# Six batches of an attention result turned by VectorE and DMA instead of TensorE, a fixed order in layer 2, and the last two groups of seven products interleaved

## The chip, the cores and the metric

The kernel runs on one core of a Trainium2 chip. The metric is device time in microseconds (us) of one execution; lower is better. The core has five engines that run side by side and wait for each other by semaphores: TensorE (PE in the profile: matrix products and transposes into PSUM), VectorE (DVE), ScalarE (ACT), GpSimd (POOL) and SyncE (SP), which here only issues transfers. Transfers that SP issues stand in one queue, in order; ScalarE can issue transfers on a queue of its own.

## The reference, cut to what matters

Four layers act on x, 8 batches of 128 tokens with 512 features, all in 32-bit floats:

```
x = x + L0_ffn(L0_cond(x))      # gated MLP with low-rank adapters, then a routed adapter layer
x = x + L1_ffn(L1_cond(x))      # adapters
x = x + L2_ffn(L2_cond(x))      # attention over a paged cache, then a mixture with 8 experts
x = x + L3_ffn(L3_cond(x))      # routed adapters, then 64 experts of rank 8, the best 16 gated
```

The change touches what follows the attention of layer 2. Attention gives y2 with tokens on the partitions; the rest of layer 2 needs it with features on the partitions:

```
H       = y2 @ W.T + b                       # 512 x 512
z       = y2 @ A                             # rank 32
weights = routing(H[anchors, :8], z[anchors] @ LiMEs.T)   # anchors: every second token
x       = x + H + (z * (weights @ LiMEs)) @ Bmat * 0.5
```

and the end of layer 3, where the gated ranks z (512 by 1024 tokens, called zgT) are multiplied by a 512 x 512 matrix and added to x, which is then the output.

## The kernel before, in words

Attention (`attention`, called through `att.run`) takes 32 steps: eight quarters of the heads (`qd`, 0 to 7), and within each four pairs of batches (`p`, 0 to 3), so step n = 4 qd + p. A step projects the next step's queries, keys and values, weighs (scores `st`, L1249, and the exponentials on ScalarE), sums and mixes (`av`, L1301). The sums of the exponentials are inverted on VectorE (`inverted`), written to memory and read back as R, spread over all partitions (L1293 and L1294 on SP); R scales `av` into oT (`divided`, L1311). One step later `leave(n - 1)` multiplies oT with the output weights (L1055, tiles wo_one, wo_two, wo_six) and adds into y2; the last sums of it are added on GpSimd (L1336, L1341), in the last step on VectorE. After the last quarter (`qd` = 7) a pair's y2 is complete when its `leave` is done: the pair p - 1 in the step of pair p.

Products of size 2 x 2 blocks are made with seven block products and sums of blocks instead of eight products (`seven`, and in the last layer the class `Seven`).

At the end of steps 29, 30 and 31 (qd = 7, p = 1, 2, 3) `end.turn` turns the two batches of the pair before: four transposes on TensorE for each batch into one PSUM bank (L1884), copied by VectorE or ScalarE to Y2T (L1885). The last two batches are turned in `layer2`. After step 31 `run` scales the last pair (`divided`), makes the sums of blocks of it (`outputs`, four VectorE sums), starts the first quarter of H on TensorE (`end.product(0, ...)`: two PSUM banks, 16 products), and then does the last `leave`. `layer2` turns batches 6 and 7, makes the anchors' logits (`anchors`, tile hdT) and z (`low`), the products for the quarters 0 to 3 of the tokens (`product`), with `routing` on VectorE beside them, and the addition to x (`added`).

An fp32 product of TensorE stands in the trace as two instructions ("passes").

A planner orders the instructions of each engine ahead of time; it may put an instruction that is ready ahead of an earlier one that is not. `kept(...)` (`tc.keep_in_program_order`) exempts an instruction from that: the kept ones of an engine stay in the order in which the program gives them. In attention nearly everything is kept; in `ending` before the change the transposes of `turn`, the products of `low`, `anchors` and `product`, and all of layer 3 are not. SP's queue within a step is, in order: the turned new keys and queries (`written`, L1204, four transfers), their loading (L1237, L1239), the sums and R (L1293, L1294), the turned cached keys (L1204) and their loading (kT, L1200). In step 30 the loads of W2 and Aw follow (L1873, L1877); after step 31 come the weights of the last two layers (`open3`, L2024 to L2041) and the sums read back for a check (L833). The tiles called kn hold gathered keys of the cache and belong to the pool `kvp`, two buffers; no keys are gathered from step 30 on.

PSUM has eight banks. In attention and layer 2 they are three with the tag st, two with av and three with mm; in layer 3 all eight have the tag mm.

At the end, `layer3` turns zgT for the second half of the tokens, begins the two last groups (`last_begun(1, k)`), makes the sums zs on VectorE and does `last(1, 0)` and `last(1, 1)`: the six remaining block products of a group (`go_on`, L2121, L2122, L2124 on VectorE between them), additions to x (L2252), and for each of the four results an addition from PSUM (L2258) and a store from SP's queue (L2259). The result blocks (0, 0) and (1, 0) of a group share one PSUM bank, (0, 1) and (1, 1) the other.

Of the kernel before, what the change touches and what calls it, by code (L numbers as in the profile page):

```python
# [47 lines left out]
def forward(ctx: ExitStack, tc: tile.TileContext, a: dict, out: bass.AP):  # L48
# [32 lines left out]
    late_turned = w3T, wB3T, A2T  # L81
# [795 lines left out]
def attention(tc, a, x, ident, lens, kvrow, part, ww, wop, ypool, sums, rot, eps, psa, c2, chunks, mm):  # L877
# [524 lines left out]
    def run(pool_, end_of, bank, keep):  # L1402
# [12 lines left out]

        def some(ops, k=1):
            return lambda: [next(ops, None) for _ in range(k)]

        for n, (qd, p) in enumerate(steps):
# [75 lines left out]
            if qd == NQ - 1 and p:  # L1495
                for j in range(2):
                    end.turn(y2, 2 * (p - 1) + j, bank)
        divided(n)
        every(outputs(n))
        end.product(0, ("st", "st"), bank)  # L1500
# [313 lines left out]
def ending(  # L1814
# [64 lines left out]
    def turn(y2, b, bank):  # L1879
        if not Y2T:  # L1880
            Y2T.append(early.tile([P, DC, NT], F32, tag="yT", name="y2T"))
        ps = bank("mm", [P, DC, P], f"y2T_{b}")
        for c in range(DC):
            pe.transpose(ps[:, c, :], y2[:, b, c * P : (c + 1) * P], ident)  # L1884
        (act.copy if b % 2 else dve.tensor_copy)(Y2T[0][:, :, b * P : (b + 1) * P], ps)  # L1885

# [3 lines left out]
    def low(bank):  # L1890

        ps = bank("mm", [P, NT // 4], "z2")
        for c in range(DC):
            for q in range(4):
                mmq(ps[slot(q), :], A2[:, c, :], Y2T[0][:, c, quarter(q)], c == 0, c == DC - 1)
        act.copy(zq, ps)

    def anchors(bank, meanwhile):

        ps = bank("mm", [P, P], "hdT")  # L1900
        for c in range(DC):
            for q in range(4):
                mmq(ps[slot(q), :], WH[:, c, :], Y2T[0][:, c, q * NT // 4 + 1 : (q + 1) * NT // 4 : 2], c == 0, c == DC - 1)
        hdT = L3.w3.tile([P, P], F32, tag="hdT", name="hdTs")
        dve.tensor_copy(hdT, ps)
        meanwhile()
        ps = bank("mm", [P, NA, 32], "hd")
        pe.transpose(ps.rearrange("p q e -> p (q e)"), hdT, ident)
        dve.tensor_tensor(hd, ps[:, :, 0:16], b16.unsqueeze(1).to_broadcast([P, NA, 16]), ALU.add)
# [8 lines left out]
    def product(q, tags, bank, at=range(2), begun=False):  # L1918

        for i, tag in zip(at, tags):  # L1920
            ps = H[q, i] if begun else bank(tag, [P, 2, NT // 4], f"h_{q}_{i}")
            for o in range(2):
                for c in range(DC):
                    mmq(
                        ps[:, o, :], W["2"][:, c, (2 * i + o) * P : (2 * i + o + 1) * P], Y2T[0][:, c, quarter(q)],
                        not begun and o == 0 and c == 0, begun and c == DC - 1,
                    )
            H[q, i] = ps
# [166 lines left out]
    class Seven:  # L2095


        def __init__(self, name, bank, A, B):
            self.A, self.B = A, B
            self.even, self.odd = (bank("mm", [P, 2, 256], f"{name}_{i}") for i in range(2))  # L2100
            self.p1, self.u = (
                L3.w3.tile([P, 256], F32, tag=f"seven_{n}", name=f"{n}_{name}", bufs=2) for n in ("p", "u")
            )
            self.c = {(0, 0): (self.even[:, 0], None), (0, 1): (self.odd[:, 1], self.u),
                      (1, 0): (self.even[:, 1], self.u), (1, 1): (self.odd[:, 0], self.p1)}
# [5 lines left out]
        def begin(self):  # L2111
            self.into(self.even[:, 0], self.A[0], self.B[0], True)
            act.copy(self.p1, self.even[:, 0])

        def go_on(self):
            a11, a12, a22, s1, s2, s3, s4 = self.A
            b11, b21, b22, t1, t2, t3, t4 = self.B
            u, p1, even, odd = self.u, self.p1, self.even, self.odd
            self.into(odd[:, 1], s1, t1, True)
            self.into(odd[:, 0], s2, t2)  # L2120
            dve.tensor_tensor(u, odd[:, 0], p1, ALU.add)  # L2121
            dve.tensor_tensor(p1, odd[:, 1], p1, ALU.add)  # L2122
            self.into(even[:, 1], s3, t3)
            dve.tensor_tensor(p1, even[:, 1], p1, ALU.add)  # L2124
            self.into(odd[:, 1], s4, b22)
            self.into(even[:, 0], a12, b21)
            self.into(even[:, 1], a22, t4)
# [111 lines left out]
    def last_begun(g, k, bank):  # L2239

        f = S["o", g, k] = Seven(f"o3_{g}_{k}", bank, S["b"][k], S["z", g])
        f.begin()

    def last(g, k):
        f = S["o", g, k]
        f.go_on()
        for (i, j), (ps, more) in reversed(f.c.items()):
# [3 lines left out]
            if more is not None:  # L2251
                dve.tensor_tensor(t, t, more, ALU.add)  # L2252
        for ij in ((1, 1), (0, 1), (0, 0), (1, 0)):
            ps = f.c[ij][0]
            o = 2 * k + ij[0]
            tok = slice(g * 512 + ij[1] * 256, g * 512 + (ij[1] + 1) * 256)
            t = x[:, o, tok]
            dve.tensor_tensor(t, ps, t, ALU.add)  # L2258
            sp.dma_start(out[o * P : (o + 1) * P, tok], t)  # L2259

    def layer2(y2, bank, do=range(NB)):

        for b in do:
            turn(y2, b, bank)
        anchors(bank, lambda: low(bank))
        where = ["mm"]
        folding = fold_scores(lambda tag, shape, name: bank(where[0], shape, name))
        if (0, 0) not in H:
# [18 lines left out]
    def layer3(bank, between=lambda behind: None):  # L2287
# [33 lines left out]
        last(1, 0)  # L2321
        last(1, 1)
# [3 lines left out]
        product=product, shifted=shifted, open3=open3, layer2=layer2, layer3=layer3,  # L2326
# [66 lines left out]
```

## Time and profile before

| what | value |
|---|---|
| median of 3 runs | 1475.64 us (1473.62 to 1477.49) |
| profiled execution | 1473.67 us |
| its span, first to last instruction | 1471.8 us |
| TensorE busy | 1459.9 us, 99% of the span |
| VectorE busy | 1066.8 us, 72% |
| GpSimd busy | 855.2 us, 58% |
| ScalarE busy | 559.0 us, 38% |
| granted clock of TensorE | 0.999 |

Busy times of engines overlap. Of the engine that is busy nearly all the time, every wait counts; idle time of the others costs nothing by itself. "L1884" is line 1884 of the kernel before the change. A number in the trace such as "[3.19 <-DMA R<-sums]" is the idle time of that engine ahead of the instruction, and what ended it.

### The profile page before, as it was taken

Reading aid. Unit: us, or ns where it says so; the run is one execution under the profiler, and the core shown is the slowest. Engines: PE = TensorE matmul, PEld = TensorE weight load, DVE = VectorE, ACT = ScalarE, POOL = GpSimd, SP = SyncE. Lnnn points to the kernel's source line nnn. Section 1 sums busy time; section 2 is a strip of 40 time slices with the busy share of each in tenths; the row PEclk is TensorE's granted clock in tenths of the full one; section 3 lists DMA queues with packets and bytes.
Section 4 is the critical chain, followed back from the end, with each engine's and each line's share of the span. In section 5 each row is a group of like instructions: output and inputs, shape, how many; then the busy total and the mean of one; then the engine's idle time right before and its main releaser. Section 6 shows DMA issues by size and latency. Waiting matters only on the chain.

```text
span 1471.8 us, 17654 instructions
## 1 busy us (share of the span) xinstructions
PE 1459.9 (99%) x5333; PEld 921.6 (63%) x5333; DVE 1066.8 (72%) x2128; ACT 559.0 (38%) x1416; POOL 855.2 (58%) x877
## 2 busy tenths in 40 slices
PE   9999999999999999999999999999999999999998
PEld 7888786455555555555565555556555555657886
DVE  4675535488878887877778787777878788875575
ACT  1111101044445544454554445455444444542110
POOL 2231104477767777777677777767777776731310
PEclk9999999999999999999999999999999999999999
DMA  7430312214655544464454456444445544343001
GB/s 244 131 76 26 73 35 70 90 39 123 178 157 165 156 121 129 150 184 129 136 151 120 126 157 184 129 137 150 117 129 155 173 137 134 115 122 99 1 9 52
DMA packets 178488, 177.02 MB, mean 120 GB/s; under 512 B 72336, under 2 KB 148208, under 8 KB 178256
## 3 DMA queue, kind: packets, MB, share of 16 engines
q1 hardware_dynamic: 160208, 138.79, 32.7%
q0 software_dynamic: 17056, 36.49, 8.0%
q8 instruction: 45, 0.74, 0.2%
q10 hardware_dynamic: 1120, 0.52, 0.1%
q14 instruction: 59, 0.48, 0.1%
HBM read 132.36 MB, written 43.11 MB: 119 GB/s over the span
## 4 chain that ended last, share of the span: by engine, by line
PE 91%; DMA 3%; DVE 3%; POOL 1%; issue 1%; ACT 0%; SPq 0%; ACTq 0%; DVEq 0%; POOLq 0%
PE st L1249 17%; PE av L1301 16%; PE g L414 9%; PE q_six L1055 8%; PE q_one L1055 5%; PE q_five L1055 5%; PE wo_two L1055 5%; PE dn L414 5%; PE wo_one L1055 4%; PE wo_six L1055 4%; PE eo_l L53 3%; PE h L1834 2%; PE z L1834 2%; PE o L1834 1%; PE midp_l L53 1%; DMA qT<-turned_new 1%
## 5 line engine op out<-in xcount | busy, mean ns | idle before, releaser
L998 POOL DMA_INDIRECT kn<-in_k_cache,kvrow_k x256 | 270.8, 1058 | 77.7 <-issue 67.1
L998 POOL DMA_INDIRECT vals<-in_v_cache,kvrow_v x256 | 273.1, 1067 | 73.6 <-issue 49.5
L1301 PE MATMUL av<-pT,vals 128*128 128x512 f32 x640 | 290.6, 593 | 0.2 <-DVE oT L1311 0.2
L1253 ACT ACTIVATE pT<-st,hide 128x512 f32<-128x512 f32 x256 | 175.9, 687 | 187.2 <-PE st L1249 187.1
L1249 PE MATMUL st<-qT,kT 128*128 128x512 f32 x512 | 236.2, 594 | 1.5 <-DMA qT<-turned_new 1.4
L1301 PEld LDWEIGHTS av<-pT,vals 128*128 128x128 f32 x640 | 121.6, 190 | 152.9 <-issue 146.9
L1154 POOL TENSOR_TENSOR vq<-q,txq 128x256 f32<-128x256 f32 x128 | 121.1, 977 | 131.5 <-ACT sqq L1128 89.9
L1249 PEld LDWEIGHTS st<-qT,kT 128*128 128x128 f32 x512 | 96.4, 190 | 111.2 <-issue 99.0
L1269 DVE TENSOR_TENSOR part<-pT 128x512 f32<-128x512 f32 x128 | 88.4, 691 | 77.6 <-ACT pT L1253 73.5
L1055 PE MATMUL q_one<-q,x 128*128 128x384 f32 x256 | 93.1, 486 | 0.0
L1128 ACT ACTIVATE sqq<-q 128x128 f32<-128x128 f32 x252 | 78.2, 310 | 11.8 <-DVE q L1104 5.1
L1055 PEld LDWEIGHTS q_one<-q,x 128*128 128x128 f32 x256 | 48.6, 190 | 39.7 <-issue 14.1
L1055 PE MATMUL q_six<-q_s,xs_all 128*128 128x384 f32 x192 | 69.8, 486 | 0.0
L1109 ACT COPY q<-q_one 128x256 f32<-128x256 f32 x32 | 11.9, 372 | 148.8 <-PE q_one L1055 142.7
L1055 PE MATMUL wo_one<-o,oT 128*128 128x256 f32 x256 | 65.7, 379 | 0.0
L1249 PE MATMUL st<-qT,kTn 128*128 128x512 f32 x128 | 65.4, 593 | 0.0
L1055 PE MATMUL wo_two<-o_s,os 128*128 128x256 f32 x256 | 60.6, 380 | 0.0
L1253 ACT ACTIVATE pT<-st,rs 128x512 f32<-128x512 f32 x64 | 44.0, 687 | 38.6 <-PE st L1249 38.6
L483 POOL TENSOR_TENSOR ws<-wu 128x256 f32<-128x256 f32 (+1 forms) x9 | 6.4, 711 | 87.7 <-DMA wu<-in_WuT 87.7
L1055 PEld LDWEIGHTS wo_one<-o,oT 128*128 128x128 f32 x256 | 48.7, 190 | 13.3 <-issue 0.5
L1285 ACT COPY rows<-rows 32x32 f32<-32x32 f32 x96 | 20.7, 216 | 93.1 <-DVE rows L1280 92.3
L414 PE MATMUL g<-xs,ws 128*128 128x256 f32 (+1 forms) x240 | 55.1, 379 | 0.0
(457 smaller groups left out, 2803.5 us busy)
## 6 DMA issues: line engine op xcount, KB each, us to landing
turned_new<-qkt SPq DMA_DIRECT2D x120, 160.0 KB
turned_cached<-kt SPq DMA_DIRECT2D x128, 128.0 KB
kT<-turned_cached SPq DMA_DIRECT2D x32, 512.0 KB
R<-sums SPq DMA_DIRECT2D x32, 512.0 KB
qT<-turned_new SPq DMA_DIRECT2D x30, 512.0 KB
q<-in_WqT SPq DMA_DIRECT2D x8, 1024.0 KB
o<-in_WoT SPq DMA_DIRECT2D x8, 1024.0 KB
kn<-in_k_cache,kvrow_k POOLq DMA_INDIRECT x256, 2.9
```

What stands on the lines that cost most here:

```text
L53: pe.matmul(o, lhsT, rhs, start=start, stop=stop)
L414: pe.matmul(o, lhsT, rhs, start=start, stop=stop, skip_group_check=True)
L998: kept(pool.indirect_dma_start(out=d[:, c, :], out_offset=None, in_=kc if what == "k" else vc, in_offset=bass.IndirectOffsetOnAxis(ap=kvro ...
L1055: kept(pe.matmul(o, l[:, c, :], r[:, c, :], start=start and c == 0, stop=c == 1, skip_group_check=True))
L1128: kept(act.activation(sq, S[n][m][:, j, i, :], AF.Square, accum_out=S[n]["ssq"][:, j, col : col + 1]))
L1154: kept(pool.tensor_tensor(to, t[:, b, :, hi : hi + 64], wx[:, b, lo : lo + 64].unsqueeze(2).to_broadcast(list(to.shape)), ALU.mult,))
L1249: kept(pe.matmul(ps, s["kT"][:, c, 4 * j : 4 * j + 4, :] if c < 4 else s["kn"][:, j], s["qT"][:, :, REP * j : REP * (j + 1), :].rearrange( ...
L1253: kept(act.activation(pT[:, c, :, :].rearrange("p i t -> p (i t)"), ps, AF.Exp, **(dict(bias=hide[:, b, c : c + 1]) if c < 4 else dict(bia ...
L1269: kept(dve.tensor_tensor(o, l, r, ALU.add))
L1285: kept(act.copy(rows[0:32, g, :], rows[32 * g : 32 * g + 32, 0, :]))
L1301: kept(pe.matmul(ps, v[:, c, :], pT[:, c, :, :].rearrange("p i t -> p (i t)"), start=c == 0, stop=c == NC - 1, skip_group_check=True,))
L1834: return pe.matmul(o, lhsT, rhs, start=start, stop=stop, skip_group_check=True)
```

## The change

1. In steps 29, 30 and 31 the batches 0 to 5 are no longer turned by TensorE. `turned_in` has VectorE turn blocks of 32 x 32 (one instruction for each batch, into a tile of the kn buffers), SP writes the blocks to a tensor in memory (four transfers a batch), and reads them back into Y2T with the features on the partitions (four transfers a batch). All are kept in order.
2. The first quarter's product after step 31 makes 12 of its 16 products ahead of the last `leave`; `layer2` makes three more, then turns batches 6 and 7 on TensorE, then makes the last one.
3. The transposes of `turn`, the products of `low` and `anchors`, and the products of `product` for the quarters 0, 1 and 2 are kept in order.
4. `Seven.go_on` is cut into `lead` (three block products and their sums) and `close` (the other three), and `last` into `summed_up` and `last_out`. The two last groups run as lead, lead, close, close.
5. In the very last group (`apart`) the result (1, 0) has a PSUM bank of its own, and its last block product, its addition and its store are made in two halves of 128 columns. In the last two groups the stores of (0, 1), and of the second half, are issued on ScalarE's queue. In every `Seven` the bank `odd` is now taken before `even`.

```diff
+    y2_turned = nc.dram_tensor("y2_turned", (NB - 2, 32, 4 * DC, 4, 32), F32, kind="Internal").ap()
...
+        def y2_turned(p):
+            bs = (2 * p, 2 * p + 1)
+            end.turned_in(y2, bs, lambda name: kvp.tile([P, 4, DC, 32], F32, tag="kn", name=name))
...
             if qd == NQ - 1 and p:
-                for j in range(2):
-                    end.turn(y2, 2 * (p - 1) + j, bank)
+                y2_turned(p - 1)
         divided(n)
         every(outputs(n))
-        end.product(0, ("st", "st"), bank)
+        end.product(0, ("st", "st"), bank, part=slice(0, 12))
         leave(n)
...
+    def turned_in(y2, bs, tile_of_turned):
+
+        if not Y2T:
+            Y2T.append(early.tile([P, DC, NT], F32, tag="yT", name="y2T"))
+        for b in bs:
+            t = tile_of_turned(f"y2t_{b}")
+            kept(dve.transpose(t, y2[:, b, :].rearrange("p (c k i) -> p k c i", k=4, i=32)))
+            for q in range(4):
+                kept(sp.dma_start(
+                    late_turned[3][b, :, :, q], t[32 * q : 32 * q + 32].rearrange("i k c j -> i (k c) j")
+                ))
+        for b in bs:
+            for k in range(4):
+                kept(sp.dma_start(
+                    Y2T[0][slot(k), :, b * P : (b + 1) * P],
+                    late_turned[3][b, :, DC * k : DC * (k + 1)].rearrange("i c a j -> i c (a j)"),
+                ))
...
+        placed = kept if q < 3 else lambda i: i
+        tags = dict(zip(at, tags))
+        for i, o, c in [(i, o, c) for i in tags for o in range(2) for c in range(DC)][part]:
+            if (q, i) not in H:
+                H[q, i] = bank(tags[i], [P, 2, NT // 4], f"h_{q}_{i}")
+            placed(mmq(
...
-            self.even, self.odd = (bank("mm", [P, 2, 256], f"{name}_{i}") for i in range(2))
+            self.odd = bank("mm", [P, 2, 256], f"{name}_1")
+            self.even = bank("mm", [P, 2, 256], f"{name}_0")
+            self.one, self.six = self.even[:, 0], (
+                bank("mm", [P, 2, 256], f"{name}_2")[:, 0] if apart else self.even[:, 1]
+            )
...
-            self.into(even[:, 1], a22, t4)
+            for h in (slice(0, P), slice(P, 2 * P)) if self.apart else (slice(0, 2 * P),):
+                self.into(six[:, h], a22, t4[:, :, h])
...
+            n = P if f.apart and ij == (1, 0) else 2 * P
+            for h in range(0, 2 * P, n):
+                by = act if g and (ij == (0, 1) or h) else sp
...
+                dve.tensor_tensor(t, ps, t, ALU.add)
+                by.dma_start(out[o * P : (o + 1) * P, tok], t)
...
+        begun = (0, 0) in H
+        if begun:
+            product(0, ("st", "st"), bank, part=slice(12, 15))
         for b in do:
             turn(y2, b, bank)
+        if begun:
+            product(0, ("st", "st"), bank, part=slice(15, 16))
         anchors(bank, lambda: low(bank))
...
-        last(1, 0)
-        last(1, 1)
+        both = [S["o", 1, k] for k in range(2)]
+        for k, f in enumerate(both):
+            f.lead()
+            summed_up(1, k)
+        for k, f in enumerate(both):
+            f.close()
+            last_out(1, k)
```

## The prediction

> **What bounds the kernel now.** I read the page's busy shares first, then TensorE's waits, then the timeline at the three places where the change takes transposes away, then SP's own queue, and last the chain and the stores at the end.
>
> ```profile
> PE 1459.9 (99%) x5333; PEld 921.6 (63%) x5333; DVE 1066.8 (72%) x2128; ACT 559.0 (38%) x1416; POOL 855.2 (58%) x877
> ```
>
> TensorE is the bound: 11.9 us of the span's 1471.8 are not matmul, and 5.9 of them lie behind the last matmul (ended about 1465.9). So a microsecond that leaves TensorE in the middle leaves the kernel, unless TensorE then meets something that is late. Its waits by releaser (total, times, longest) are small:
>
> ```profile
> PE st L1249 <- DMA qT<-turned_new: 1.4, 3, 0.5
> ...
> PE o L1834 <- DVE p_o L2122: 0.2, 1, 0.2
> ```
>
> The timeline around the turns of y2 (columns: start, length, engine, line, operation, tiles, count):
>
> ```profile
> 1270.64 1.04 PE L1884 MATMUL y2T<-ident,y 128*128 128x128 f32 x8
> 1271.52 3.60 PE L1249 MATMUL st<-qT,kT 128*128 128x512 f32 x8
> ...
> 1303.76 1.04 PE L1884 MATMUL y2T<-ident,y 128*128 128x128 f32 x8
> 1304.63 3.60 PE L1249 MATMUL st<-qT,kT 128*128 128x512 f32 x8
> ...
> 1328.30 1.04 PE L1884 MATMUL y2T<-ident,y 128*128 128x128 f32 x8
> 1329.18 7.07 PE L1834 MATMUL h<-y2T,WT 128*128 128x256 f32 x32
> ...
> 1332.83 1.29 DVE L1311 TENSOR_TENSOR oT<-av,R 128x512 f32<-128x512 f32 x2 [3.19 <-DMA R<-sums]
> ```
>
> See in it that eight transposes hold TensorE for 0.88, 0.87 and 0.88 us (start to next start), and that behind the third lies the first product of layer 2 (32 passes, 6.91 us, 0.216 each), which covers the wait for R: oT is there at 1334.12, TensorE comes to it (wo_one) at 1336.09. SP's queue:
>
> ```profile
> 1278.09 0.34 SPq L1200 DMA_DIRECT2D kT<-turned_cached  x1
> 1293.68 1.87 SPq L1204 DMA_DIRECT2D turned_new<-qkt  x4
> ...
> 1327.23 0.34 SPq L1293 DMA_DIRECT2D sums<-inv  x1
> 1328.63 0.34 SPq L1294 DMA_DIRECT2D R<-sums  x1
> 1329.08 1.76 SPq L2030 DMA_DIRECT2D Bm<-in_Bmat  x4
> ```
>
> There are holes in it of 15 us here and of 22 us ahead of sums<-inv, just where the new transfers come. The end, by the chain and by the stores' tile view (issue min/median/max in ns):
>
> ```profile
> 1463.06 2.87 PE o L1834 x12
> ...
> 1465.95 0.44 DVE x L2258
> ```
> ```profile
> L2259 SPq DMA_DIRECT2D out<-x x16: 332/360/1541, 1432.5 to 1467.4; - x16
> ```
>
> The last four stores sit on SP from 1464.89 to 1467.82, one of them for 1.54 us; the span ends 4.0 us later.
>
> **The change part by part.** Times are those of the profiled execution: 1473.67 us, span 1471.8 and 1.9 around it. It is 1.97 below the median of the runs (1475.64); I carry the difference over to the median.
>
> *A, B: the turns in steps 29 and 30.* Sixteen transposes leave TensorE: -0.88 and -0.87. The record of each is 273 ns long, but eight follow within 0.88 us (0.11 each), and the spacing is what counts. The Trainium skill, TensorE: Matmul & The Clock Gate, Part 4: PE-mode transpose, gives about 275 ns for one in a kernel's context; by that the 24 transposes would be worth an estimated 6.6 us instead of 2.63. The record's length agrees with it, the spacing does not.
> What is added is beside the path. VectorE: two transposes of 128x512 a step (row of kt<-kn: 0.71 each) for one copy of 0.68 gone, net +0.74; in step 29 the first sum of pT moves from 1274.16 to about 1274.5, and the hole of 1.02 us before the next sum takes that in; ScalarE loses a copy of 0.58. SP: 8 writes and 8 reads a step. The writes have the form of the weights' turning (w_turned<-late, 64 KB in 128-byte pieces: eight in 4.15 us, 0.52 each; the next use of their buffer 1.57 us after the last), the reads that of Bm (0.44 each). Step 29: kT's load is issued at 1278.43, writes to 1282.6, reads to about 1288; the next in the queue, turned_new, waits for VectorE until 1293.68. Cover 5 us. Step 30: behind W2 and Aw (2 MB; the transfers last to about 1314), writes landed by 1318, reads issued by 1320; next is sums<-inv at 1327.23. Cover 7 us. Bounds for each: -0.88, and -0.35 if the scores then wait for qT (longest such wait 0.5). qT is issued at 1266.29, 4.35 before TensorE would arrive; I take the whole.
>
> *C: the turn in step 31 and the order in layer 2.* Eight transposes go (-0.88) and four products of the first group (8 passes) move behind the last output group. TensorE now has 24 x 0.216 = 5.17 us between 1328.30 and the output group, so to 1333.47. oT's first half is there at 1333.48: wo_one, 0.86, to 1334.34. The second factor needs oT whole (1334.12) and two sums of 0.42: 1335.05. A wait of about 0.7 us that was covered by the eight passes. They are done later (12 to 15 while VectorE adds the last results to y2, the last one after the transposes), a place where the order of before put eight passes too, of product 1. So -0.88 + 0.70 - 0.07 = -0.25. Bounds: -0.88 (wait covered), and above by the y2 of batches 4 and 5 coming late, the second rival.
> That transfer: VectorE turns at 1327.2 to 1328.7, inside its 3.19 us wait for R; SP writes behind R's issue, 1328.97 to 1333.1, landed by 1336.5 behind R's 512 KB; reads to 1338.3, landed 1340. The first use, product hdT of layer 2, comes at: output group from 1335.05 (24 passes left, 5.17) to 1340.3, then 6 passes, eight transposes, 2 passes: 1342.9. Cover 3 us. The layer's loads (Bm to sums, 9.6 us on SP from 1329.08) move back to 1338 to 1346; the first user, product qwp at 1357.55, has 11 us.
>
> *D: the last two groups interleaved.* From the first product on zs (1454.60), 48 passes are 10.37 us, plus 0.28 until VectorE can read: 1465.25, while VectorE starts at 1465.95. TensorE waited 0.70: about half for the sums zs, half for u and p_o before the fourth product of a group. With the second group's lead between, the latter goes. -0.55; bounds -0.70 and 0. Dividing the last product in halves adds no columns.
>
> *E: the stores.* Before, VectorE's two last adds begin together, since both results lie in one bank (0.76), then SP: from 1465.95 to the last issue's end 1467.82 are 1.87 us. After, the bank is another one, (0,0) is added during the last product, and the end is one 128x128 add (0.28 as in vals<-q_six), a hop of 0.05 and one issue on ScalarE's queue of 0.40: 0.73. -1.14, and a half store (64 KB) lands somewhat earlier; R's chain shows 1.4 us for 4 KB, so I take -0.26. E = -1.40. Bounds: -0.6 if the 1.54 us issue is no part of a usual run (0.6 of the gain is its), 0 if such an issue falls on the new last store, and -1.9.
>
> Sum: -0.88 - 0.87 - 0.25 - 0.55 - 1.40 = -3.95: 1469.7 for the profiled execution, 1471.7 for the median. That is 0.27%; a measurement of this kernel can tell about 0.3% (4.4 us) from no change.
>
> **The rivals.**
> 1. *The end keeps its length* (1473.2 to 1473.9). The 1.54 us issue meets the new last store, or it was a single run's. For it: SP has seven other issues over 1.4 us. Against: the new last store is alone on its queue. Gain 2.6, or 3.3 without E's 0.6. The Trainium skill, DMA: Bandwidth & Descriptors, Issuing engines are not separate DMA queues, says that issuing from several engines saves only the sequencer's issue time; by that the second queue would give E an estimated 0.4 and the rest of E comes from the adds. The long issue here is issue time too, and no run shows yet which.
> 2. *Layer 2 waits for y2 of batches 4 and 5* (slower). If the layer's loads stand on SP between the writes and the reads, the reads begin at 1333.1 + 9.6 = 1342.7, end 3.5 later and land at 1347.8; hdT stands in front of every product of the layer in the now fixed order and waits 4.9 us: 1475.64 - 3.95 + 4.9 = 1476.6. It decides when the reads land 3.95 after 1342.9. Against: the loads did not slip ahead of sums and R before, though SP stood idle from 1305.5 to 1327.2.
> 3. *R late.* If step 30's reads still hold SP at 1326, sums<-inv slips by as much, and TensorE, already waiting 0.7, by the same. 7 us of cover speak against it; with 12 us of delay it would be 1476.7.
> 4. *The transposes cost their records' length* (24 x 0.273 = 6.55): 1467.8. The 0.11 us spacing speaks against it.
> 5. *Other order in layer 3.* Its products are left to the planner, and Seven now takes its banks in another order; a wait like fp's or z's on VectorE (0.2) ten times would be 2 us: 1473.7.
>
> **How the numbers follow.** Forecast (gain 2.7 to 5.2) 0.62, of which 0.35 lies beyond 4.4 with the runs' own spread of 1.9 to either side; a larger gain (C's wait covered, or rival 4) 0.08; rival 1 0.12; rival 2 0.08, its harder half over 0.3%; rival 3 0.05; rival 5 0.05. Faster 0.44, within 0.3% 0.46, slower 0.10. Range: below, all lower bounds, -0.88 - 0.87 - 0.88 - 0.70 - 1.9 = -5.2, and 1.1 for the spread of a median: 1469.3. Above, rivals 2 and 3: 1476.8.
>
> **What would show it.** Right: no y2T transposes but eight, near the end of attention; scores at once behind av in steps 30 and 31; about 0.7 us idle before wo_one or wo_two of the last step, on oT; no wait of the o products on p_o; the last add 128 wide, less than 5.1 us (now) before the end. Wrong: hdT waiting for a DMA on y2T; SP's y2 reads behind Bm or W; sums<-inv held by SP; a long issue on ScalarE at the end.

## The result, and the profile after

The changed kernel takes 1473.68 us (median of 22 runs, 1470.99 to 1478.27). The kernel before, run beside it, takes 1476.19 (22 runs). The ratio is 0.9983, 95% interval 0.9977 to 0.9990. That is 2.5 us less where I had forecast 3.95; it is inside the range, nearer to its middle than to the forecast, and a little over half of the 0.3% that I had called the bound, though the interval is clear of no change. The profiled execution took 1473.39 us, its span 1471.5.

The two profiled spans differ by only 0.28 us, and that difference cannot be read as it stands. Ahead of every changed instruction the second profile is already 2.01 us late: the scores of step 28 begin at 1257.77 before and at 1259.78 after. Their code is the same. In the twelve profiles of the experiments below, whose code is the same up to there, they begin at 1256.78 to 1260.84; so this is what one execution differs from another. I compare local stretches from here on.

TensorE in the timeline after (start, length, engine, line, operation, tiles, shape, count; the idle time in brackets):

```profile
1259.78 2.74 PE L1250 MATMUL st<-qT,kT 128*128 128x512 f32 x6
...
1272.66 3.60 PE L1250 MATMUL st<-qT,kT 128*128 128x512 f32 x8
...
1292.02 2.74 PE L1250 MATMUL st<-qT,kT 128*128 128x512 f32 x6
...
1304.90 3.60 PE L1250 MATMUL st<-qT,kT 128*128 128x512 f32 x8
...
1328.57 5.34 PE L1838 MATMUL h<-y2T,WT 128*128 128x256 f32 x24
1333.75 1.10 PE L1056 MATMUL wo_one<-o,oT 128*128 128x256 f32 x4
1335.23 1.99 PE L1056 MATMUL wo_two<-o_s,os 128*128 128x256 f32 x8 [0.39 <-DVE os L1015]
...
1340.52 1.46 PE L1838 MATMUL h<-y2T,WT 128*128 128x256 f32 x6
1341.81 1.04 PE L1888 MATMUL y2T<-ident,y 128*128 128x128 f32 x8
1342.69 0.60 PE L1838 MATMUL h<-y2T,WT 128*128 128x256 f32 x2
1343.21 1.30 PE L1838 MATMUL hdT<-y2T,WH 128*32 128x128 f32 x31
...
1356.82 0.60 PE L2011 MATMUL pT<-ident,p 128*8 128x128 f32 x4
...
1454.47 5.66 PE L1838 MATMUL o<-zs,Bws 128*128 128x256 f32 x24
...
1464.29 1.05 PE L1838 MATMUL o<-zs,BwT 128*128 128x128 f32 x8
```

The same places before:

```profile
1257.77 2.74 PE L1249 MATMUL st<-qT,kT 128*128 128x512 f32 x6
...
1290.88 2.74 PE L1249 MATMUL st<-qT,kT 128*128 128x512 f32 x6
...
1356.95 0.60 PE L1987 MATMUL pT<-ident,p 128*8 128x128 f32 x4
...
1454.60 3.50 PE L1834 MATMUL o<-zs,Bws 128*128 128x256 f32 x14
```

From the first line after to the second are 12.88 us; before it was 13.75 (1257.77 to 1271.52). From the third to the fourth are again 12.88, where it was 13.75 (1290.88 to 1304.63). TensorE's lateness against before is 2.01 us, then 1.14, then 0.27 at step 31's scores, -0.13 at pT in layer 2 (1356.95 before), still -0.13 at the last groups' products on zs (1454.60 before), and -0.57 at the end of the last matmul (1465.34 against 1465.91). So A gave 0.87, B 0.87, C about 0.39 (0.26 or 0.27 to -0.13), and D 0.44.

SP's queue after, from its timeline:

```profile
1282.61 5.37 SPq L1899 DMA_DIRECT2D y_turned<-y2t  x8
1288.14 3.83 SPq L1904 DMA_DIRECT2D y2T<-y_turned  x8
1294.82 1.26 SPq L1205 DMA_DIRECT2D turned_new<-qkt  x3
...
1306.73 12.42 SPq L1899 DMA_DIRECT2D y_turned<-y2t  x8
1319.32 4.14 SPq L1904 DMA_DIRECT2D y2T<-y_turned  x8
...
1327.49 0.31 SPq L1294 DMA_DIRECT2D sums<-inv  x1
1328.84 0.35 SPq L1295 DMA_DIRECT2D R<-sums  x1
1329.28 5.54 SPq L1899 DMA_DIRECT2D y_turned<-y2t  x8
1334.98 3.82 SPq L1904 DMA_DIRECT2D y2T<-y_turned  x8
1338.91 1.75 SPq L2054 DMA_DIRECT2D Bm<-in_Bmat  x4
```

All three turns fit into the holes. The tightest is step 29: the writes begin only behind kT's load, which stands 2.07 us later against the scores of step 28 than before, and 2.85 us are left between the end of the reads (1291.97) and turned_new. In step 30, behind the 2 MB of W2 and Aw, the eight writes take 12.42 us to issue, and 4.0 us are left between the end of the reads (1323.46) and sums<-inv. The last turn stands ahead of Bm, and hdT waits for no transfer.

The gain is lost behind the last matmul. From its end to the span's end were 5.87 us; now they are 6.17. VectorE's timeline and the stores' tile view after:

```profile
1465.38 0.49 DVE L2306 TENSOR_TENSOR x<-o,x 128x128 f32<-128x128 f32 x2 [0.47 <-PE o L1838]
```
```profile
L2307 SPq DMA_DIRECT2D out<-x x14: 332/384/1369, 1432.4 to 1466.1; - x14
L2307 ACTq DMA_DIRECT2D out<-x x3: 338/362/373, 1462.3 to 1465.9; - x3
```

The last addition ends 0.52 us behind the last matmul (0.79 before), the last issue 1.15 behind it (1.91 before). But by the trace's records of transfers the last packet of a store came 3.69 behind it, where it was 3.36. A gain of 0.76 at the issue has turned into a loss of 0.33 at the landing. Both halves of the last result are added behind the last matmul: VectorE waits 0.47 us and adds the first half 0.04 us after the second half's matmuls have ended, so the halves brought nothing forward.

Two more things stand at the end of the program. The kernel ends with a branch: each engine loads a flag and, if it is set, everything would be computed again (it is not, in any run). The line view of this branch before, with its code's next instruction on each engine (an engine's name with q is its sequencer, PEldq is TensorE's; durations in ns; then the start):

```profile
L850 ACTq COMPARE_BRANCH  x1: 50/50/50, 1455.3 to 1455.3; - x1
L850 ACTq EVENT_SEMAPHORE  x1: 17/17/17, 1457.9 to 1457.9; - x1
L850 PEldq COMPARE_BRANCH  x1: 3578/3578/3578, 1464.3 to 1464.3; - x1
...
L850 DVEq EVENT_SEMAPHORE  x1: 21/21/21, 1469.8 to 1469.8; - x1
```

and after:

```profile
L851 PEldq COMPARE_BRANCH  x1: 3782/3782/3782, 1462.7 to 1462.7; - x1
...
L851 ACTq COMPARE_BRANCH  x1: 54/54/54, 1467.0 to 1467.0; - x1
L851 DVEq EVENT_SEMAPHORE  x1: 21/21/21, 1469.1 to 1469.1; - x1
L851 ACTq EVENT_SEMAPHORE  x1: 17/17/17, 1470.3 to 1470.3; - x1
```

ScalarE had passed its branch 8 us ahead of the last matmul's end. Now its branch stands behind the last store on its queue, and it goes on only at 1470.3, 3.3 us later. TensorE's sequencer, which runs ahead of its array, reached the branch 1.58 us ahead of the last matmul's end before, and 2.60 ahead of it after. In both kernels, 1.0 to 1.1 us behind that branch, and again 4.5 us behind it, a single transfer of 16 KB runs on the instruction queue for 1.1 to 1.3 us. The second of these after lies at 1467.30 to 1468.59; the transfers in just that window:

```profile
DMA  9733110100000000901910000000000000000001
...
q1 hardware_dynamic: 69, 0.03, 7.7%
q8 instruction: 1, 0.02, 6.2%
```

One packet on q8 takes 6.2%, all the time of one of the 16 DMA engines; the others have nothing left of the stores to do in most of the window. Of the stores' packets that began from 1 us ahead of the last matmul's end on, 90% were there at 1.95 behind it; the last few come at up to 3.69, 0.44 behind the end of this load.

### The profile page after: what moved, and what is told of

The parts are those of the page before. It is cut to its first block, busy times and chain, and to the rows that moved or that the text cites. A ratio compares the mean times of both kernels' runs of the same rounds, so it can differ in the third digit from the quotient of the medians.

```text
span 1471.5 us, 17701 instructions
## 1 busy us (share of the span) xinstructions
PE 1458.0 (99%) x5313; PEld 918.8 (62%) x5313; DVE 1067.8 (73%) x2132; ACT 557.5 (38%) x1413; POOL 855.5 (58%) x877
## 4 chain that ended last, share of the span: by engine, by line
```

## The experiments

The question was where E went. Three theories stood first. T1: the branch at the end, with the loads of instructions that it brings, sets how long the end is. T2: the traffic of the stores themselves does (more of them at once, on two queues). T3: the profiled executions were not usual ones. In what follows "+x" is x us behind the end of the last matmul. The groups of experiments ran on different chips, so each is compared with the kernel before that ran beside it.

### The two halves of the change

tail_alone is the kernel before with parts 4 and 5 of the change, turn_alone with parts 1, 2 and 3.

```diff
 # tail_alone, in part
+        for k, f in enumerate(both):
+            f.lead()
+            summed_up(1, k)
+        for k, f in enumerate(both):
+            f.close()
+            last_out(1, k)
...
+                by = act if g and (ij == (0, 1) or h) else sp
```
```diff
 # turn_alone, in part
+                y2_turned(p - 1)
...
+        end.product(0, ("st", "st"), bank, part=slice(0, 12))
...
+            kept(pe.transpose(ps[:, c, :], y2[:, b, c * P : (c + 1) * P], ident))
```

> The kernel before with the change's last two parts alone (the two last groups interleaved, stores on two queues). Theory 1, the end-of-program branch: around the branch TensorE's instruction loads (16 KB each) hold up one issue on SP and the packets of the last store, and they move with the end, so the stores' gain is not paid out: D -0.45 stays, E is -0.3 to +0.3; time -0.2 to -0.8 us, span from the last product's end to the end of the span 5.6 to 6.2 us as in the kernel before (5.9) and after (6.2). Theory 2, the stores get in each other's way on the 16 DMA engines: the same numbers. Theory 3, the profiled run of the changed kernel was not typical and the gain is there in most runs: -1.9 us, 4.5 us from the last product to the end.

Measured: 1476.18 us (12 runs) beside 1476.16 before, ratio 0.9998 (0.9989 to 1.0007). In its profile the last issue ends at +1.12 and the last packet comes at +2.59, earlier than in either kernel; but the span ends at +6.36. Its line view of the branch:

```profile
L850 SPq EVENT_SEMAPHORE  x8: 17/17/17, 1470.4 to 1472.1; - x8
...
L850 ACTq COMPARE_BRANCH  x1: 54/54/54, 1470.2 to 1470.2; - x1
L850 DVEq EVENT_SEMAPHORE  x1: 21/21/21, 1472.4 to 1472.4; - x1
L850 ACTq EVENT_SEMAPHORE  x1: 17/17/17, 1473.9 to 1473.9; - x1
```

SP has its stores landed at +3.30 and then waits for ScalarE's semaphore, which comes with the last line, at +5.39. So here ScalarE's late branch ends last, and the span ends 0.97 behind it.

> The kernel before with the turning of six batches, the cut product and the kept order alone; the end as before. By the profiles' local differences (0.87, 0.87 and 0.39 us) -2.1 us under theories 1 and 2; under theory 3 the whole of -2.5 would be made up of -1.9 at the end and only -0.6 here.

Measured: 1473.60 us (12 runs), ratio 0.9986 (0.9976 to 0.9996), so 2.1 us less by the ratio and 2.6 by the medians; A, B and C in the timeline of after make 2.13. Its end is as before (+5.81, with an SP issue of 1577 ns). What the change gains is gained by the turns; interleaving and stores together gain nothing that these runs can tell (the interval reaches from 1.6 us less to 1.0 more).

### Without the branch

These two leave out the loading of the flag, the branch and the recomputation behind it.

```diff
-    redo = nc.values_load(redo_i[0:1, 0:1], min_val=0, max_val=1)
-    with tc.If(redo > 0):
-        sp.dma_start(x, kept)
-        ...
```

> The kernel before without the branch at its end (left out: the attention done over again when a sum of exponentials is out of range; the sums are still checked). Theory 1: no 16 KB instruction load near the last stores, no SP issue over 0.6 us there; 0.5 to 2.5 us faster than the kernel before. Theory 2: the long issue on SP stays, since it comes from the stores.

> The changed kernel without that branch (the same left out). Theory 1: the gain of E comes out here: 3.4 to 4.0 us less than the kernel before without the branch (2.1 for the turning, 0.45 for the order of products, 0.9 to 1.4 for the stores), and 1.2 us or more less than the kernel before's from the last product to the end. Theory 2: the stores still block each other, 2.1 to 2.7 us less.

Measured: before without it 1473.93 us (12 runs, ratio 0.9985, 0.9976 to 0.9994), after without it 1471.11 (9 runs, 0.9968, 0.9957 to 0.9979). The difference is 2.82 us by the medians and 2.5 by the ratios. The first lies between what T1 (3.4 to 4.0) and T2 (2.1 to 2.7) expected, the second within T2's, so the times alone don't decide between them. The stores' tile view of before without the branch:

```profile
L2233 SPq DMA_DIRECT2D out<-x x16: 332/366/389, 1431.9 to 1466.2; - x16
```

The long issue (1541 ns) is gone, with all its stores in place and in the same order; nor is there a load of instructions at the end. That speaks against T2 for the long issue, and against T3: it comes back in turn_alone. In after without the branch two much earlier issues of stores, near 1433, still take 0.50 and 1.11 us; a 16 KB load on the instruction queue runs during both. Without the branch the end is +3.78 for before and +3.24 for after. Of the 2.09 us that before's end loses, 1.03 lie ahead of the last packet (+3.36 to +2.33) and 1.06 behind it (2.51 us to 1.45), so loads that hold packets are not all that the branch costs. Between the two kernels, E is worth 0.54, 0.36 of it at the last issue and 0.17 at the landing (last packet +2.33 and +1.80). One reason that it isn't 1.40: some 0.6 of that was the long issue, and that leaves the kernel before too when the branch goes.

### Whose branch: ScalarE's

Theory 4: ScalarE's late branch made the end longer. Theory 5: TensorE's loads of instructions hold the last store's packets, on whichever queue it is issued. Three kernels differ from the changed one in the stores alone:

```diff
 # one_queue
-                by = act if g and (ij == (0, 1) or h) else sp
+                by = sp
 # last_on_sp
-                by = act if g and (ij == (0, 1) or h) else sp
+                by = act if g and ij == (0, 1) else sp
 # late_scalar: one_queue, and
                 by.dma_start(out[o * P : (o + 1) * P, tok], t)
+                if g and h:
+                    act.copy(f.u[:, 0:1], t[:, 0:1])
```

> The changed kernel with all stores issued by SP, the order of the last groups and the divided last result kept. From the last matmul's end to the span's end it was 5.87 us before, 6.17 after, 6.36 with the interleaving and the two queues alone; in the latter two ScalarE loads the flag and takes the final branch only behind its last store (at +0.98 and later), where it did so 11 us ahead of the last matmul's end before. Theory 4 (ScalarE's late branch lengthens the end): its load and branch are back ahead of the last matmul, and the end is 5.2 to 5.6 us, set by VectorE's branch (about 0.55 to 3.8) and SP's last landing; the median is 0.6 to 0.9 under the changed kernel's, 0.9973 to 0.9979 of before. Theory 5 (the last store's packets are late because TensorE's instruction load runs on the same DMA engines, whichever queue issues them): 6.0 to 6.4, and the median as after or later, 0.9983 to 0.9990.

> The changed kernel with the last half store on SP; ScalarE keeps the two stores ahead of it. ScalarE is free for its branch about 1.5 us earlier than after. Theory 4: the end is 5.2 to 5.7 us from the last matmul, SP's issues end as early as after (about +0.95 to +1.15), the median 0.5 to 0.9 us under the changed kernel's. Theory 5: 6.0 to 6.4, no gain.

> All stores on SP, and a copy of one column by ScalarE behind VectorE's last addition, which nothing reads: ScalarE's branch is held back without any store moved. Theory 4: ScalarE's load and branch come at about +0.9 again and the end is 6.1 to 6.4 us from the last matmul, as after, 0.5 to 0.9 longer than with all stores on SP without the copy. Theory 5: as long as with all stores on SP without the copy, within 0.2.

Measured, beside 1473.95 before (27 runs): one_queue 1471.79 (ratio 0.9986, 0.9977 to 0.9995), last_on_sp 1471.61 (0.9987, 0.9978 to 0.9996), late_scalar 1471.39 (0.9984, 0.9975 to 0.9994), 11 runs each. With ScalarE's branch early again (-10.1, and +0.06 with the last store on SP) the profiled ends are +6.25 and +6.29: theory 4 fails as the cause in the changed kernel; theory 5's 6.0 to 6.4 is what came. ScalarE's branch is only next in line there: with its 0.97 behind ScalarE's +4.97 it would end the span at about +5.9 if the packets were early. In after itself SP comes to its wait for ScalarE only at +5.21, behind its waits for the stores, when ScalarE's semaphore has been there since +4.99. In late_scalar the end is +7.30, which neither expected: there SP's very last issue was held for 2077 ns, while TensorE's second load ran for 1.73. Its median is no worse than the others', so such an end is one execution's, not every one's.

### TensorE's branch moved

If theory 5 holds, it is the time of TensorE's branch that counts. First I took the halves of the last result away, on the idea that they had brought the branch forward:

```diff
-            for h in (slice(0, P), slice(P, 2 * P)) if self.apart else (slice(0, 2 * P),):
-                self.into(six[:, h], a22, t4[:, :, h])
+            self.into(six, a22, t4)
...
-            n = P if f.apart and ij == (1, 0) else 2 * P
+            n = 2 * P
 # no_halves
+                by = act if g and ij == (0, 1) else sp
 # no_halves_scalar
+                by = act if g and (ij == (0, 1) or f.apart and ij == (1, 0)) else sp
```

> The changed kernel with the last product and the last result undivided (256 columns, in a bank of their own) and the last store on SP. In the runs so far the first half's addition began only 0.04 us behind the second half's last matmul, so the halves gave nothing; with them TensorE's final branch came 2.60 us ahead of its last matmul's end (1.58 before), and its loads of instructions at about -1.5 and +2.0 instead of -0.6 and +2.9; the second one held the last store's packets until +3.7 to +4.0. Theory 5 (those loads hold the stores): without halves they are back at about -0.6 and +2.9; the last addition ends at +0.47, an SP issue at -0.4 is held to about +0.6, the last one ends at 1.0 to 1.1, the last packet comes at 1.9 to 2.6, SP's wait for the landing ends by 3.2, and VectorE's branch (3.85) sets the end: 5.0 to 5.3 us from the last matmul, 0.9 to 1.3 less than with halves and the last store on SP (6.29). Rival 6 (the packets are late because of any load behind a branch, VectorE's and ScalarE's too, wherever TensorE's fall): 5.8 to 6.3.

> The same without halves, but the last store on ScalarE's queue, so that ScalarE's final branch is behind it. Theory 4b (a late branch of ScalarE holds the end by itself, once the landings are early): landings as without halves and the last store on SP (by 3.2), but ScalarE's first instruction behind its branch comes at 4.9 to 5.4 and SP waits for it: 5.9 to 6.4 us. If ScalarE's branch costs nothing: 5.0 to 5.3, as with the last store on SP.

Measured beside 1474.62 before (21 runs): no_halves 1472.40 (11 runs, ratio 0.9976, 0.9967 to 0.9985), no_halves_scalar 1472.00 (11 runs, 0.9984, 0.9975 to 0.9993). The idea was wrong in its sign: TensorE's branch came earlier still, at -3.44. In each profile so far with the interleaving and the branch 17 matmuls start behind TensorE's load of the flag, halves or not; before it were 9. Undivided they last longer, so the branch is further ahead. The loads came at -2.42 and at +1.60 to +2.74. In no_halves the last issue ended at +0.82, the last packet came at +3.39, 0.65 behind the load's end, and the span ended at +5.77: better than after, by less than theory 5 expected (5.0 to 5.3), and next to the 5.8 to 6.3 of rival 6, by which any load behind a branch makes the packets late. In no_halves_scalar the load ran to +3.21, the last packet came at +4.25, and the end at +6.60. Its late landing ended last, so it tells nothing of ScalarE's branch by itself.

Then I held TensorE's branch back and moved no store, by a transpose behind the last product that nothing reads:

```diff
 # both on no_halves; held_early
+        at = 512 + 0 * 256
+        pe.transpose(both[0].odd[:, 0, 0:P], x[:, 1, at : at + P], ident)
 # held_late
+        at = 512 + 0 * 256
+        pe.transpose(both[0].odd[:, 0, 0:P], x[:, 2, at : at + P], ident)
```

> The changed kernel without halves and with the last store on SP (5.77 us from the last matmul to the span's end), and one transpose of 128x128 behind TensorE's last product, whose result nothing reads and which waits for VectorE's last result of the other group (ends at -1.80). It holds TensorE's final branch back from -3.44 to about -1.2, and moves no store. Theory 5 (TensorE's second load of instructions, about 4.5 to 5 us behind its branch, holds the last store's packets; a store that meets none lands 1.5 us behind its issue, as before, and with the interleaving and the two queues alone): the loads come at about -0.1 to +1.0 and from +3.3 on; the last issue ends at 0.8 to 1.4, the last packet comes at 2.3 to 2.9 instead of 3.39, and the end is 4.8 to 5.4 us, so 0.4 to 0.9 less; about 0.9972 of before. Rival 6 (the packets are late because of any load behind a branch): 5.7 to 6.2.

> The same, with the transpose waiting for VectorE's last result but one (ends at -0.40), so that TensorE's branch comes at about +0.15 and its first load at about +1.2 to +2.4, upon the last store's packets again. Theory 5: the last packet comes 0.4 to 1.1 us behind that load's end, 2.8 to 3.4, and the end is 5.2 to 5.9 us, 0.3 to 0.7 more than with the earlier hold. If the place of TensorE's loads is nothing to the stores: within 0.2 of the earlier hold.

Measured beside 1477.03 before (23 runs): held_early 1473.33 (12 runs, ratio 0.9977, 0.9965 to 0.9989), held_late 1474.06 (12 runs, 0.9978, 0.9967 to 0.9988). In the profiles, counted from the last product and not from the transpose 0.11 behind it, TensorE branched at -1.15 and at +0.55. In held_early its first load ran from -0.14 to +1.59, longer than expected, and SP's last issue fell into it:

```profile
L2306 SPq DMA_DIRECT2D out<-x x14: 332/383/1471, 1432.5 to 1465.9; - x14
```

The longest of these is the last one; it ended at +1.96, and its last packet came 1.42 later, at +3.38. The end is +5.76 and not 4.8 to 5.4; by this number alone it would be rival 6's (5.7 to 6.2). But the packets followed the issue by the 1.5 us of theory 5, and it was the issue that came late. In held_late the same issue took 332 ns and ended at +0.82, but the first load then lay upon its packets, from +1.56 to +3.34. The transfers from 1466.7 to 1468.5, the stretch of that load:

```profile
DMA  9965211000000900000000000000000000000002
...
q1 hardware_dynamic: 73, 0.06, 10.1%
q8 instruction: 1, 0.02, 6.2%
```

The last packet came at +4.24, 0.90 behind the load's end, and the span ended at +6.64: 0.88 more than with the earlier hold, by the place of the load alone. That is theory 5's case (0.3 to 0.7 expected; 0.2 at most if the place of the loads were nothing to the stores), as these two profiles show it, one of each kernel; the medians are too coarse to confirm 0.9 us. Rival 6 stays open in part: smaller loads (8 KB each, on q14) run in the same stretches, and no run has TensorE's loads alone.

All profiles together, in us behind the end of the last product:

```
                   TensorE    its loads                  last issue  last    span
                   branches   1st          2nd           ends        packet  ends
before             -1.58      -0.57 +0.57  +2.93 +4.01   +1.91       +3.36   +5.87
turn_alone         -1.58      -0.55 +0.60  +2.97 +4.18   +1.95       +3.50   +5.81
tail_alone         -2.59      -0.81 +0.11  +2.69 +3.71   +1.12       +2.59   +6.36
after              -2.60      -1.53 -0.25  +1.96 +3.25   +1.15       +3.69   +6.17
one_queue          -2.60      -1.48 -0.45  +2.02 +3.22   +1.87       +3.91   +6.25
last_on_sp         -2.60      -1.35 -0.38  +1.81 +3.26   +1.73       +3.99   +6.29
late_scalar        -2.60      -1.58 -0.42  +2.02 +3.75   +4.08       +4.94   +7.30
whole              -2.60      -1.50 -0.43  +2.30 +3.30   +0.95       +3.99   +6.53
no_halves          -3.44      -2.42 -1.07  +1.60 +2.74   +0.82       +3.39   +5.77
no_halves_scalar   -3.40      -2.39 -0.65  +1.51 +3.21   +0.88       +4.25   +6.60
held_early         -1.15      -0.14 +1.59  +3.85 +4.98   +1.96       +3.38   +5.76
held_late          +0.55      +1.56 +3.34  +5.61 +6.57   +0.82       +4.24   +6.64
before_no_branch   -          -            -             +1.30       +2.33   +3.78
after_no_branch    -          -            -             +0.94       +1.80   +3.24
```

With the branch the span ends 2.3 to 2.55 us behind the last packet in eleven of twelve; the twelfth is tail_alone, which waited for ScalarE. The profile does not say for which engine a load is; that these are TensorE's is read from their times: the first begins 1.0 to 1.25 us behind TensorE's branch in eleven of the twelve, while that branch moves over 4 us. In before, turn_alone, tail_alone and held_early the last packet comes 1.42 to 1.55 us behind the last issue. In the seven others that store in time (after, one_queue, last_on_sp, whole, the two without halves, held_late) a load begins before such 1.5 us are over, and the last packet comes 0.4 to 1.05 behind that load's end, so 2.0 to 3.4 behind the issue. Two profiles don't follow so simple a rule: in before and turn_alone the second load begins 0.4 to 0.5 us ahead of the last packet and doesn't hold it. And in tail_alone the loads come 0.7 us later behind the same branch than in after, for a reason that no run shows.

### The cut of layer 2's first product

```diff
-        end.product(0, ("st", "st"), bank, part=slice(0, 12))
+        end.product(0, ("st", "st"), bank)
...
-        if begun:
-            product(0, ("st", "st"), bank, part=slice(12, 15))
...
-        if begun:
-            product(0, ("st", "st"), bank, part=slice(15, 16))
```

> The changed kernel with all sixteen products of layer 2's first group ahead of attention's last output group again, and none behind it. If cutting four of them off is worth what my sum has it at (a wait of 0.4 to 0.7 us before the output group, against their 0.86 us filling TensorE's time behind it while VectorE adds the last results): no wait on VectorE's oT or os before wo_one and wo_two, but TensorE idles 0.4 to 0.9 us before the transposes of the last two batches or before hdT, and from the last scores to the product hdT it takes as long as after or up to 0.5 us longer. If the places behind the output group were not idle anyway: the same stretch is 0.4 us shorter than after.

Measured in one profile (1475.24 us), TensorE's timeline:

```profile
1329.11 7.07 PE L1838 MATMUL h<-y2T,WT 128*128 128x256 f32 x32
1336.01 1.03 PE L1056 MATMUL wo_one<-o,oT 128*128 128x256 f32 x4
...
1343.46 0.88 PE L1888 MATMUL y2T<-ident,y 128*128 128x128 f32 x6 [1.02 <-DVE y L1342]
1344.27 1.74 PE L1838 MATMUL hdT<-y2T,WH 128*32 128x128 f32 x31
...
1358.31 0.60 PE L2011 MATMUL pT<-ident,p 128*8 128x128 f32 x4
```

No wait before wo_one or wo_two, and 1.02 us of idle time before the last transposes, for the last sums of y2. From the last scores of step 31 (1321.38) to hdT are 22.89 us; after it was 22.37 (1320.84 to 1343.21). hdT itself then takes 1.74 us instead of 1.30: no product is left to fill the time until Y2T is copied (at 1344.96). To pT are 36.93 us, after it was 35.98, and before 36.37 (1320.58 to 1356.95). So by one profile of each the cut of the product is worth 0.95 us in the changed order, and without it this stretch would be 0.56 longer than in the kernel before: the cut is what makes C a gain.

### The best of them

no_halves has the lowest ratio of those that keep the branch, 0.9976 (0.9967 to 0.9985), and held_early 0.9977, against 0.9983 (0.9977 to 0.9990) for the changed kernel. The medians of no_halves and its before give only 0.9985. The intervals overlap, so it beats the kernel before, and the changed one only by appearance.

## Why the prediction was right, and where it was wrong

The time is in the range and the direction is right; the likeliest case did not come. The working gave -0.88, -0.87, -0.25, -0.55 and -1.40. The profile has -0.87, -0.87, -0.39, -0.44 and +0.30: -2.27 in place of -3.95, and the medians say -2.5. A to D together came to -2.57 where I had -2.55; that close a sum is luck in part, since C came out 0.14 better and D 0.11 worse. What is missing is E.

- **A and B** are right in size and mechanism. The spacing of 0.11 us was what each transpose cost, and not its record's 0.273. The Trainium skill, TensorE: Matmul & The Clock Gate, Part 4: PE-mode transpose, has about 275 ns for one: the records agree with it, and the time that came back when eight were taken away, 0.87 us, does not. The fourth rival falls with that.
- **C** is right in its mechanism. The wait was there, on os behind oT: from wo_one to wo_two are 1.48 us instead of 0.86, so 0.62 where I had 0.70. That is 0.08 of the 0.14 by which C came out better (the sum also has a term of -0.07 for which I showed no row); the rest is less than such a wait differs between profiles (0.39 here, 0.24 in one_queue).
- **The second rival** did not come: the reads of y2 stood ahead of Bm on SP, and hdT came with no wait. **The third** did not come either, though its cover was 4.0 us and not 7 (and step 29's 2.85 and not 5): the writes behind the 2 MB took three times the 4.15 us that I had taken from the weights' turning. They were the same writes, but in a full stretch. **The fifth** did not come: between pT and the last groups the two kernels take the same time to 0.01 us.
- **D** is right: the wait for p_o is gone, and a wait for zs is left (0.2 in the list of waits).
- **E is the step that failed.** I had it as "-1.14, and a half store (64 KB) lands somewhat earlier", with 0 as the bound on the side of a loss. The issue did come 0.76 earlier; the landing, which I had left to follow the issue by a fixed time, came 1.09 us later behind it. I had read the 1.54 us issue as something that stores do, and not looked at what else moved at that time: the loads of instructions that TensorE's branch starts. They decide the end in two ways, by holding an issue (before, turn_alone, held_early, late_scalar) or by holding the last packets (after and the rest). The interleaving of D brought TensorE's branch 1.0 us forward (tail_alone has it too), and in the changed kernel that put the second load onto the last store: so the gain at the issue was lost. I take it that the wait for p_o had held the sequencer: before, it ended at 1463.06, 2.85 us ahead of the last matmul's end, with twelve matmuls still to come, all of them ahead of the branch in its order. That a wait holds the branch back is what held_early and held_late show (-1.15 and +0.55 instead of -3.44). What is shown is that the packets are late where the load lies, and that they move with it when only TensorE's branch is moved. Why a load of one packet holds a few packets of a store is not shown; that they stand behind it on the same DMA engine fits the 6.2%, but the records don't name the engine.
- The halved last result was part of E's 1.14 and gave nothing of its own, since both additions began behind the last matmul.
- **The first rival**, "the end keeps its length", gave 1473.2 to 1473.9, and that is where the time is. I had given it 0.12. My range for it did not follow from its own gains, 2.6 or 3.3, which make 1473.0 or 1472.3 from 1475.64; the measured gain is 2.5. Its reason was not quite the one that came: the long issue did not meet the new last store (1369 ns on the third last, at 1464.11). The sentence of the Trainium skill, DMA: Bandwidth & Descriptors, Issuing engines are not separate DMA queues, that stood beside it holds here: two queues instead of one (one_queue against after) brought the last issue from +1.87 to +1.15, 0.72 where I had estimated 0.4 by it, and the last packet only from +3.91 to +3.69.

## What to carry to other kernels

Where a kernel ends in a branch, read what the loads of instructions do in the last microseconds before you shorten anything there: a shorter way to the last store is worth nothing if its packets then meet such a load, and moving a store to another engine's queue moves that engine's branch behind it. Count the end in three times, last issue, last packet and end of the span, and not in one. In the middle of a kernel whose TensorE never rests, count a transpose by what it adds to the spacing, and pay for its replacement out of holes in the queues that the timeline shows.

## What the runs showed of the hardware

- Among the last nine stores of each profile an issue on SP's queue took 0.33 to 0.42 us, but for 0.64 once in last_on_sp and thirteen of 0.78 to 2.08; a 16 KB load of instructions ran during each of the thirteen. Without the branch, and so without loads at the end, none took over 0.41. Not every issue during a load was long: one of 0.38 us began at -1.71 in after, and ScalarE's at -0.89 took 0.36 there and 0.59 in no_halves_scalar. Nor does every long issue have a load: of the seven others over 1.4 us in before, three have one, and four, at 9 to 42 us, have none.
- An engine that reaches a branch late pays for it: ScalarE's next instruction came 3.3 us behind its branch in after and 3.8 in tail_alone, VectorE's 3.1 in before and after and 4.2 in whole. Reached early, it costs nothing that the end sees.
- TensorE's sequencer loaded the flag with up to 17 matmuls still to start and came to the branch with 15, and the first load of instructions began while those matmuls ran.
- Eight writes of 64 KB in pieces of 128 bytes took 5.4 us to issue on a free queue and 12.4 behind 2 MB of loads.
